# Slots of four samples in place of two, stores of 2 MB in place of 1 MB, and a first round of loads split over two DMA queues

## The chip, the core and the metric

The kernel runs on one core of one Trainium2 chip, in one launch. The metric is device time in microseconds (us). The kernel before was timed in three runs: 326.96, 327.68 and 327.71 us, median 327.68 us.

A core has a matrix engine (TensorE, "PE" in the profile, its weight loads "PEld"), a vector engine ("DVE"), an activation engine ("ACT"), a general engine ("POOL") and a synchronisation engine ("SP"). Here SP and ACT compute nothing: they only wait on semaphores and issue DMA transfers. A transfer issued by SP goes through queue q1 of the profile, one issued by ACT through queue q10. Both queues are worked off by the same 16 DMA engines. Each of the 16 adds one to the transfer's semaphore when its share has landed, so a finished transfer adds 16 (`DMA = 16` in the code).

## The reference

There are 128 samples. Each sample `x[b]` is a float32 matrix of 128 channels by 1024 time steps, 512 KB. A subject number from 0 to 7 picks one of eight 128x128 weight matrices for each sample, and the sample's product with it is added to the sample:

```
w = weights[subjects]                       # (128, 128, 128)
out = x + einsum('bct,bcd->bdt', x, w)      # (128, 128, 1024), float32
```

So 64 MB are read and 64 MB are written, with 512 KB of weights beside them. Every sample is used once.

## The kernel before

**Tiling.** The 128 samples are taken in 64 tiles of `G = 2` samples, 1 MB each. The on-chip memory holds `SLOTS = 23` slots `xs[k]`, one tile each. Tile `i` uses slot `i % 23`. Within a slot the 128 partitions are the channels, and a partition's row holds the two samples' 1024 floats one after the other, 8 KB.

**Loads.** SP first loads all eight weight matrices (L132), then runs over the tiles (L133 to L145) and issues one transfer of 512 KB for each sample. A load is written so that four rows of a sample, 16 KB that lie together in memory, are read as one piece and written into four partitions (`ROWS = 4`, L144). In the first round, from the fourth tile on, SP waits until the tile three places back has landed (`LEAD = 3`, L138). In later rounds SP waits until the slot's earlier tile has been stored (L136). A slot has one semaphore, which counts two loads and one store a round (`TURN`).

**Compute.** For each sample POOL copies the weight matrix that the subject picks into one of four small buffers (L170). For the first sample of a tile, the copy first waits until the vector engine has finished the tile two places back (L169), and until the tile's two loads have landed (L172). Then PE multiplies the sample in two pieces of 512 time steps into one of two PSUM buffers (L177; each float32 matmul shows as two instructions). When both samples of a tile are done, DVE adds the PSUM buffer to the slot in place (L187), 128x2048 elements in one instruction.

**Stores.** ACT waits for the add of tile `i` (L188) and issues one transfer of 1 MB for it (L189 to L194): 128 rows of 8 KB, each of which goes to two places in memory, 4 KB for each sample. The order of the work on every engine is the order written in the source; there is no planner. The two loops are written one after the other, but each engine only sees its own instructions, so SP runs ahead as far as its waits and its queue let it. At the end SP waits until the last 23 stores have landed (L197, L198).

The helper `transfer` (L52) issues every load and store, so that in the profile all of them bear its line, L59.

Of the kernel before, what the change touches and what calls it, by code (L numbers as in the profile page):

```python
# [1 line left out]

# [4 lines left out]

F32 = mybir.dt.float32
I32 = mybir.dt.int32
ALU = mybir.AluOpType


G = 2  # L30

N = 512

SLOTS = 23

W_SLOTS = 4
P_SLOTS = 2

R = 8
DMA = 16  # L40

TURN = DMA * (G + 1)

LEAD = 3

IDLE = 3

ROWS = 4
QUEUES = {mybir.EngineType.SP: "qSPDynamicHW", mybir.EngineType.Activation: "qActDynamicHW"}


def transfer(nc, engine, out, in_):  # L52

    later, nc._always_lower_symbolic_ap = nc._always_lower_symbolic_ap, False
    ins, outs = engine.lower_ap_dma(in_), engine.lower_ap_dma(out)
    nc._always_lower_symbolic_ap = later
    return engine.add_instruction(  # L59
        mybir.InstDMACopy(  # L60
            name=nc.get_next_instruction_name(),
            engine=engine.engine,
            ins=ins,
            outs=outs,
            mode="Copy",
            cce_op=ALU.bypass,
            queue=QUEUES[engine.engine],
        )
    )


@with_exitstack
def kernel(
    ctx: ExitStack,
    tc: tile.TileContext,
    x: bass.AP,
    subjects: bass.AP,
    weights: bass.AP,
    out: bass.AP,
):  # L80
    nc = tc.nc
    B, C, T = x.shape
    S, _, D = weights.shape
    NT = B // G

    def sbuf(name, *shape, dtype=F32):
        return ctx.enter_context(nc.sbuf_tensor(name, list(shape), dtype)).ap()

    given, near, wrap, index = (
        sbuf(name, 1, B, dtype=I32) for name in ("given", "near", "wrap", "index")  # L90
    )
    w_all = sbuf("w_all", C, S, D)
    ws = [sbuf(f"w{i}", C, 1, D) for i in range(W_SLOTS)]
    zeros = sbuf("zeros", C, N)
    xs = [sbuf(f"x{i}", C, G, T) for i in range(SLOTS)]
    ps = [
        ctx.enter_context(nc.psum_tensor(f"ps{i}", [D, G, T], F32)).ap() for i in range(P_SLOTS)
    ]

    s_given = tc.alloc_semaphore("s_given")  # L100
    s_wall = tc.alloc_semaphore("s_wall")
    s_index = tc.alloc_semaphore("s_index")
    s_zeros = tc.alloc_semaphore("s_zeros")
    s_copied = tc.alloc_semaphore("s_copied")
    s_product = tc.alloc_semaphore("s_product")
    s_added = tc.alloc_semaphore("s_added")
    s_slot = [tc.alloc_semaphore(f"s_slot{i}") for i in range(SLOTS)]

    with tc.tile_critical():  # L109

        nc.scalar.dma_start(given, subjects.rearrange("(o b) -> o b", o=1)).then_inc(s_given, DMA)

        nc.vector.memset(zeros, 0.0).then_inc(s_zeros, 1)  # L113
        nc.tensor.wait_ge(s_zeros, 1)
        for _ in range(IDLE):
            nc.tensor.matmul(  # L116
                ps[P_SLOTS - 1][:, G - 1, :N], zeros[:, :D], zeros, start=True, stop=True
            )

        nc.vector.wait_ge(s_given, DMA)
        nc.vector.tensor_scalar(near, given, -S, S - 1, ALU.max, ALU.min).then_inc(s_index, 1)  # L123
        nc.vector.wait_ge(s_index, 1)
        nc.vector.tensor_scalar(wrap, near, 0, S, ALU.is_lt, ALU.mult).then_inc(s_index, 1)  # L125
        nc.vector.wait_ge(s_index, 2)
        nc.vector.tensor_tensor(index, near, wrap, ALU.add).then_inc(s_index, 1)  # L127
        nc.gpsimd.wait_ge(s_index, 3)

        nc.sync.dma_start(w_all, weights.rearrange("s c d -> c s d")).then_inc(s_wall, DMA)  # L132
        for i in range(NT):  # L133
            k, turn = i % SLOTS, i // SLOTS
            if turn:
                nc.sync.wait_ge(s_slot[k], TURN * turn)  # L136
            elif i >= LEAD:
                nc.sync.wait_ge(s_slot[k - LEAD], DMA * G)  # L138
            for g in range(G):
                transfer(  # L140
                    nc,
                    nc.sync,
                    xs[k][:, g, :],
                    x[i * G + g].rearrange("(a r) t -> a (r t)", r=ROWS),  # L144
                ).then_inc(s_slot[k], DMA)  # L145

        nc.gpsimd.wait_ge(s_wall, DMA)
        for i in range(NT):
            k, turn = i % SLOTS, i // SLOTS
            loaded = TURN * turn + DMA * G  # L150
            p = ps[i % P_SLOTS]

            if i < P_SLOTS:
                nc.tensor.wait_ge(s_slot[k], loaded)
            for g in range(G):
                b = i * G + g
                if b % R == 0:
                    _, subject = nc.values_load_multi_w_load_instructions(  # L160
                        index[0:1, b : b + R],
                        engines=[mybir.EngineType.Pool],
                        min_val=0,
                        max_val=S - 1,
                        skip_runtime_bounds_check_because="the index is clamped on the chip above",
                    )
                w = ws[b % W_SLOTS]
                if i >= P_SLOTS and g == 0:
                    nc.gpsimd.wait_ge(s_added, i - P_SLOTS + 1)  # L169
                copy = nc.gpsimd.tensor_copy(w, w_all[:, bass.ds(subject[b % R], 1), :])  # L170
                if i >= P_SLOTS and g == 0:
                    copy.wait_op(s_slot[k], loaded, "sem-ge")  # L172
                copy.then_inc(s_copied, 1)

                nc.tensor.wait_ge(s_copied, b + 1)
                for t in range(0, T, N):
                    mm = nc.tensor.matmul(  # L177
                        p[:, g, t : t + N],
                        w[:, 0, :],
                        xs[k][:, g, t : t + N],  # L180
                        start=True,
                        stop=True,
                    )
                mm.then_inc(s_product, 1)

            nc.vector.wait_ge(s_product, (i + 1) * G)
            nc.vector.tensor_tensor(xs[k], p, xs[k], ALU.add).then_inc(s_added, 1)  # L187
            nc.scalar.wait_ge(s_added, i + 1)  # L188
            transfer(  # L189
                nc,  # L190
                nc.scalar,
                out[i * G : (i + 1) * G].rearrange("g d t -> d g t"),
                xs[k].rearrange("d (o g) t -> d o (g t)", o=1),
            ).then_inc(s_slot[k], DMA)  # L194


        for i in range(NT - SLOTS, NT):  # L197
            nc.sync.wait_ge(s_slot[i % SLOTS], TURN * (i // SLOTS + 1))  # L198


# [1 line left out]
_INS = ["x", "itok_B_0_7", "L0_cond_weights"]  # L202
_OUTS = [((128, 128, 1024), "float32")]


# [20 lines left out]
```

## Time and profile before

| | |
|---|---|
| median of three runs | 327.68 us |
| the profiled execution's own time | 327.88 us |
| its span, from first to last instruction | 326.0 us |
| PE busy | 239.9 us (74%) |
| DVE busy | 147.9 us (45%) |
| POOL busy | 34.4 us (11%) |
| queue q1 (SP): packets, bytes, share of the engines' time | 7184, 67.64 MB, 49.6% |
| queue q10 (ACT): packets, bytes, share of the engines' time | 9218, 67.11 MB, 49.1% |
| one load, median from issue to landing | 11.8 us |
| one store, median from issue to landing | 42.4 us |

The span is cut by the profile into 40 equal slices of 8.15 us; for each slice it gives the busy share of the engines and of the 16 DMA engines in tenths, and the bytes moved in GB/s. The same numbers can be asked of the trace for any stretch of time. A packet is what a DMA engine moves in one go; the small packets of 4 bytes that raise a semaphore are counted too. Times inside the execution, such as "at 276 us", count from the start of the span. MB and GB in the profile are decimal; the "512 KB" and "2 MB" of a transfer are 524,288 and 2,097,152 bytes.

### The profile page before, as it was taken

The page shows a single profiled execution, that of the slowest core. Times are in us where ns is not written, and L with a number is a line of the kernel's source. Part 1 is how long each engine was busy: PE and PEld are TensorE (multiplying, and loading weights), DVE is VectorE, ACT ScalarE, POOL GpSimd, SP SyncE. Part 2 cuts the span into 40 slices and gives each one's busy share as a digit, 9 for nine tenths or more (in the row PEclk, how much of TensorE's full clock was granted, in tenths as well). Part 3 has the DMA queues.
Part 4 walks back from the last instruction along what each step waited for, and adds up shares of the span by engine and source line. Part 5 has one row for each costly group of instructions (what it writes and reads, how often), then busy time and mean ns, then how long its engine had stood idle before and what let it go on. Part 6 is the DMA issues. An engine that isn't in the chain of part 4 may idle for free.

```text
span 326.0 us, 1641 instructions
## 1 busy us (share of the span) xinstructions
PE 239.9 (74%) x518; PEld 95.3 (29%) x518; DVE 147.9 (45%) x68; POOL 34.4 (11%) x132
## 2 busy tenths in 40 slices
PE   5999999889898897899988988986866777000000
PEld 2444444333333332333333333332322322000000
DVE  1267667555555554555555555554354354100000
POOL 1011111111111111011111111111011010000000
PEclk9799999999999999999999999999999999555555
DMA  7999999999999999999999999999999999999993
GB/s 257 416 415 423 429 426 420 421 422 428 420 424 429 421 428 419 427 424 425 425 425 427 417 424 423 429 428 419 425 429 433 420 417 427 425 425 427 424 428 167
DMA packets 16410, 134.85 MB, mean 414 GB/s; under 512 B 3089, under 2 KB 4114, under 8 KB 4114
## 3 DMA queue, kind: packets, MB, share of 16 engines
q1 hardware_dynamic: 7184, 67.64, 49.6%
q10 hardware_dynamic: 9218, 67.11, 49.1%
q8 instruction: 4, 0.07, 0.1%
q14 instruction: 4, 0.03, 0.0%
HBM read 67.63 MB, written 67.11 MB: 413 GB/s over the span
## 4 chain that ended last, share of the span: by engine, by line
PE 43%; DVE 19%; issue 18%; POOL 2%; DMA 2%; POOLq 1%; SPq 0%
PE ps L177 43%; DVE x L187 19%; POOL w L170 2%; DMA x<-in_x_dram 2%; POOLq L170 1%; SPq L59 0%; SPq L132 0%; SPq L222 0%; SPq L109 0%
## 5 line engine op out<-in xcount | busy, mean ns | idle before, releaser
L177 PE MATMUL ps<-x,w 128*128 128x512 f32 x512 | 235.3, 606 | 34.5 <-POOL w L170 32.5
L187 DVE TENSOR_TENSOR x<-ps,x 128x2048 f32<-128x2048 f32 x64 | 146.7, 2292 | 128.7 <-PE ps L177 128.7
L177 PEld LDWEIGHTS ps<-x,w 128*128 128x128 f32 x512 | 93.6, 191 | 176.2 <-issue 95.8
L170 POOL COPY w<-w_all 128x128 f32 x128 | 34.2, 297 | 237.9 <-DMA x<-in_x_dram 197.1
L116 PE MATMUL ps<-zeros 128*128 128x512 f32 x6 | 4.6, 922 | 1.7 <-DVE zeros L113 1.7
L116 PEld LDWEIGHTS ps<-zeros 128*128 128x128 f32 x6 | 1.7, 304 | 3.7 <-issue 2.1
L113 DVE MEMSET zeros<- 128x512 f32 x1 | 0.5, 485 | 1.1 <-SPq L109 1.1
L123 DVE TENSOR_SCALAR near<-given 1x128 int32<-1x128 int32 x1 | 0.2, 215 | 0.6 <-DMA given<-in_itok_B_dram 0.6
L127 DVE CUSTOM_DVE_ANT_0 index<-near,wrap 1x256 uint16<-1x256 uint16 x1 | 0.3, 280 | 0.0
L125 DVE TENSOR_SCALAR wrap<-near 1x128 int32<-1x128 int32 x1 | 0.2, 215 | 0.0
L213 POOL MEMSET const-float32-0.0<- 128x1 f32 x1 | 0.1, 100 | 0.2 <-issue 0.2
L213 POOL MEMSET const-bfloat16-1.0<- 128x1 bf16 x1 | 0.1, 103 | 0.0
L213 POOL MEMSET const-uint8-127<- 128x1 uint8 x1 | 0.1, 102 | 0.0
L213 POOL MEMSET const-float32-1.0<- 128x1 f32 x1 | 0.1, 100 | 0.0
## 6 DMA issues: line engine op xcount, KB each, us to landing
x<-in_x_dram SPq DMA_DIRECT2D x128, 512.0 KB, 11.8
out_dram<-x ACTq DMA_DIRECT2D x64, 1024.0 KB, 42.4
w_all<-in_L_cond_weights_dram SPq DMA_DIRECT2D x1, 512.0 KB, 4.2
given<-in_itok_B_dram ACTq DMA_DIRECT2D x1, 0.5 KB
```

What stands on the lines that cost most here:

```text
L113: nc.vector.memset(zeros, 0.0).then_inc(s_zeros, 1)
L116: nc.tensor.matmul(ps[P_SLOTS - 1][:, G - 1, :N], zeros[:, :D], zeros, start=True, stop=True)
L123: nc.vector.tensor_scalar(near, given, -S, S - 1, ALU.max, ALU.min).then_inc(s_index, 1)
L125: nc.vector.tensor_scalar(wrap, near, 0, S, ALU.is_lt, ALU.mult).then_inc(s_index, 1)
L127: nc.vector.tensor_tensor(index, near, wrap, ALU.add).then_inc(s_index, 1)
L170: copy = nc.gpsimd.tensor_copy(w, w_all[:, bass.ds(subject[b % R], 1), :])
L177: mm = nc.tensor.matmul(p[:, g, t : t + N], w[:, 0, :], xs[k][:, g, t : t + N], start=True, stop=True,)
L187: nc.vector.tensor_tensor(xs[k], p, xs[k], ALU.add).then_inc(s_added, 1)
L213: nc = _bacc.Bacc("TRN2", target_bir_lowering=False, num_devices=1)
```

## The change

A slot now holds four samples (`H = 2` halves of `G = 2`), and there are 12 slots: 24 MB in place of 23. A partition's row in a slot is 16 KB. There are 32 slot fillings in place of 64.

Compute stays in halves of two samples: 64 groups of matmuls and 64 adds of 128x2048 elements, in the same order, with the same two PSUM buffers.

Stores: the first slot filling is stored in its two halves, 1 MB each; every later one in a single transfer of 2 MB, issued when its second half has been added. So there are 33 stores in place of 64. A row of the 2 MB store is 16 KB and goes to four places of 4 KB.

Loads: still one transfer of 512 KB for each sample. In the first round SP loads all four samples of slot 0, and only three samples of slots 1 to 11. The fourth samples of those eleven slots are loaded by ACT: two as soon as the weights have landed, one after each half store of slot 0, then two after each later store until none is left. The wait that kept SP at most three tiles ahead in the first round (`LEAD`) is gone. In later rounds SP loads all four samples after the slot's store has landed.

Semaphores: a slot has two, one for each half. A load counts for its half, a store for the second half (for the first filling also for the first).

```diff
-SLOTS = 23
+H = 2
+SLOTS = 12
-TURN = DMA * (G + 1)
-LEAD = 3
...
-    NT = B // G
+    NT = B // (G * H)
...
-    xs = [sbuf(f"x{i}", C, G, T) for i in range(SLOTS)]
+    xs = [sbuf(f"x{i}", C, H * G, T) for i in range(SLOTS)]
...
-    s_slot = [tc.alloc_semaphore(f"s_slot{i}") for i in range(SLOTS)]
+    s_pair = [[tc.alloc_semaphore(f"s_pair{i}_{h}") for h in range(H)] for i in range(SLOTS)]
+
+    def emptied(i, h):
+        turns = i // SLOTS
+        loads = DMA * G * turns
+        if h == H - 1:
+            return loads + DMA * turns
+        return loads + (DMA if i and i % SLOTS == 0 else 0)
+
+    def loaded(i, h):
+        return emptied(i, h) + DMA * G
+
+    def load(engine, i, q):
+        k, h = i % SLOTS, q // G
+        transfer(
+            nc,
+            engine,
+            xs[k][:, q, :],
+            x[i * H * G + q].rearrange("(a r) t -> a (r t)", r=ROWS),
+        ).then_inc(s_pair[k][h], DMA)
+
+    def store(i, q0, q1):
+        k, b = i % SLOTS, i * H * G
+        transfer(
+            nc,
+            nc.scalar,
+            out[b + q0 : b + q1].rearrange("g d t -> d g t"),
+            xs[k][:, q0:q1, :].rearrange("d (o g) t -> d o (g t)", o=1),
+        ).then_inc(s_pair[k][(q1 - 1) // G], DMA)
...
         for i in range(NT):
-            k, turn = i % SLOTS, i // SLOTS
-            if turn:
-                nc.sync.wait_ge(s_slot[k], TURN * turn)
-            elif i >= LEAD:
-                nc.sync.wait_ge(s_slot[k - LEAD], DMA * G)
-            for g in range(G):
-                transfer(
...
+            k = i % SLOTS
+            if i >= SLOTS:
+                nc.sync.wait_ge(s_pair[k][H - 1], emptied(i, H - 1))
+                if k == 0:
+                    nc.sync.wait_ge(s_pair[k][0], emptied(i, 0))
+            for q in range(H * G - (1 if 0 < i < SLOTS else 0)):
+                load(nc.sync, i, q)
+
+        shared = list(range(1, SLOTS))
+
+        def share(count):
+            for _ in range(count):
+                if shared:
+                    load(nc.scalar, shared.pop(0), H * G - 1)
+
+        nc.scalar.wait_ge(s_wall, DMA)
+        share(2)
...
-        for i in range(NT):
+        for j in range(NT * H):
+            i, h = j // H, j % H
+            k = i % SLOTS
+            p = ps[j % P_SLOTS]
+            mine = xs[k][:, h * G : (h + 1) * G, :]
...
-            nc.vector.tensor_tensor(xs[k], p, xs[k], ALU.add).then_inc(s_added, 1)
-            nc.scalar.wait_ge(s_added, i + 1)
-            transfer(
...
+            nc.vector.tensor_tensor(mine, p, mine, ALU.add).then_inc(s_added, 1)
+
+            if i == 0 or h == H - 1:
+                nc.scalar.wait_ge(s_added, j + 1)
+                store(i, h * G if i == 0 else 0, (h + 1) * G)
+                share(1 if i == 0 else 2)
```

The waits of POOL, PE and DVE are the same as before, with `j` for the tile's number and the half's semaphore for the slot's; the last waits of SP cover the last 12 stores.

## The prediction

> **What bounds the kernel now.** I read the page first: busy shares, slices, queues.
>
> ```profile
> PE   5999999889898897899988988986866777000000
> DMA  7999999999999999999999999999999999999993
> GB/s 257 416 415 423 429 426 420 421 422 428 420 424 429 421 428 419 427 424 425 425 425 427 417 424 423 429 428 419 425 429 433 420 417 427 425 425 427 424 428 167
> q1 hardware_dynamic: 7184, 67.64, 49.6%
> q10 hardware_dynamic: 9218, 67.11, 49.1%
> ```
>
> The DMA engines are full from the second slice to the last but one, at about 425 GB/s; PE stops six slices before the end. The bound is bytes: 134.85 MB at 0.425 MB/us is 317 us of the 326. The rest is the start (the first slice) and the landing at the end. The packet counts tell the packet sizes: a load is 32 packets of 16 KB and 16 small ones for the semaphore, (32+16)x128 = 6144, and the weights (1024 rows and 16) make 7184. A 1 MB store is 128 packets of 8 KB and 16 small ones: 144x64 = 9216.
>
> Then three stretches in the DMA view: loads alone, both queues full, stores alone.
>
> ```profile
> q1 hardware_dynamic: 522, 5.70, 100.7%
> ...
> q1 hardware_dynamic: 2328, 25.45, 60.4%
> q10 hardware_dynamic: 2329, 16.93, 40.4%
> ...
> q10 hardware_dynamic: 2807, 20.45, 101.4%
> ```
>
> The first line is 5 to 19 us: 407 GB/s. The next two are 100 to 200 us: the queues moved the same number of packets, 2328 and 2329, but not the same bytes. So an engine takes one packet from each queue in turn, small ones included. Three loads (144 packets, 1.5 MB) go with one store (144 packets, 1 MB): 25.45/16.93 = 1.50. The last line is 272 to 320 us: 426 GB/s from stores alone. Because loads win, they run ahead until all 23 slots are full; SP then waits for stores, and at 276 us, when the last add starts, (321-276)x0.425 = 19 MB of stores are still to move. That backlog hides the last tile's compute completely. The timeline prices what it hides (start, duration; the last number is idle time before):
>
> ```profile
> 262.13 0.53 POOL L170 COPY w<-w_all 128x128 f32 x2 [3.69 <-DMA x<-in_x_dram]
> 262.48 3.70 PE L177 MATMUL ps<-x,w 128*128 128x512 f32 x8 [0.52 <-POOL w L170]
> 266.22 2.29 DVE L187 TENSOR_TENSOR x<-ps,x 128x2048 f32<-128x2048 f32 x1 [1.93 <-PE ps L177]
> ```
>
> From a landed pair to its finished add: 268.51-262.13 = 6.4 us.
>
> **What the Trainium skill says.** "DMA: Bandwidth & Descriptors", section "Queues, rings and completion order": each engine goes round the queues that have work, one packet at a time; 2328 against 2329 agrees. Section "Issuing engines are not separate DMA queues": a second issuing engine saves only issue time. True here for the total rate, 424 GB/s with two queues and 426 with one, but the trace shows that the queue and the packet size set who gets the bytes. Section "Bandwidth": the fabric's ceiling is 435 GB/s; 426 is 98% of it, so a better packet form can gain 2% at the very most.
>
> **The change, part by part.**
>
> *Bytes, PE, DVE and POOL work* stay the same: 64 adds of 2.29 us, the same matmuls and copies.
>
> *Packets.* A store's row is 16 KB in one piece on chip, and the loads show that a 16 KB piece travels as one packet, so I take a 2 MB store as 128+16 packets. That removes 31x144 = 4464 packets, 279 on each engine. No row prices one. The skill's section "Why small descriptors are slow" gives about 3 cycles of overhead a packet, and its bandwidth section 850 MHz: 3.5 ns, an estimate of 1.0 us. Lower bound: nothing, since loads in 16 KB packets (407 GB/s) show no better rate than 8 KB stores (426). Upper bound, if stores reach the ceiling: 67 MB at 435 in place of 426 GB/s is 3.3 us. I take -0.7.
>
> *The start.* Two loads on ACT's queue at 5 us run beside SP's: 4 loads, 2.1 MB, at 425 in place of 407 GB/s: -0.2 us. They may delay the second pair of slot 0 by 2 us, but PE needs it only after its first group, which at the start takes 13.6-8.2 = 5.4 us. With `LEAD` gone SP fills its queue earlier; the order of loads is the same, so nothing.
>
> *Who gets the bytes.* This decides. 144 packets of a 2 MB store now go with three loads, 2.10 against 1.57 MB: a round is 3.67/0.425 = 8.64 us, and stores win. So the backlog no longer grows; does any remain at the end?
>
> - Fill. PE sets the pace of compute: two adds start at 13.61 and 17.04 us, 3.43 us apart, so filling 4 is added by 16+9x3.43 = 47 us; the ACT queue, full from the first store's first packet (19.9 us before: queue q10 moved one packet between 15 and 20 us), is not empty. It works off two 1 MB halves (each with three loads: 2.62/0.425 = 6.2 us), nine shared loads (each beside one of SP's: 2.5 us) and stores 1 to 4 (8.64 each): 12.3+22.2+34.5 = 69 us, done at 89. SP meanwhile: about 10 loads before 19.9, then 6+9+12 = 37 in all, 4+11x3. Both finish the fill together.
> - After it. Store n ends at 89+8.64(n-4), so store 11 starts at 141. Loads come at 3 in 8.64 us: filling n is loaded at 89+11.52(n-11). From its last packet to its store's first packet I count 0.6 (landing: before, q1's last packet moved by 271.5 us and the copy that waited for it started at 271.99) +6.4+1.1 (the weights' issue at 0.96 to first bytes at 2.1) = 8.2 us. Filling 11 is ready at 97, its store's turn comes at 141: a lag of 44 us, and each filling takes 11.52-8.64 = 2.88 off it. It is gone after 15 fillings, at the 26th of 0 to 31, about 264 us. From there stores wait for compute, a filling takes 4.19/0.425 = 9.87 us, and the last load ends at 264+4.8x9.87 = 311 us. SP never lacks a slot in this: stores are ahead.
> - The end. Filling 30 was loaded at 311-9.9 = 301.5, its store starts at 309.7 and by 311.4 has 4/7 of the rate: 0.4 MB. The remaining 1.7 MB keep the engines busy until 315.4. Store 31 can start at 311.4+8.2 = 319.6. The engines stand idle for 4.2 us, then move 2.1 MB alone in 4.9. If store 30 starts later, as the first store of before did behind queued loads (issued 15.93, first bytes 19.9, that is 4.0 in place of 1.1 us), idle is 1.2+2.1 = 3.3. If both last steps took 4 us: about 6. I take +4.2.
>
> This idle time is what the 19 MB hid before. Queued behind the last waits: ACT's last store stands behind the last add, and SP's final wait behind its landing. Earlier ACT waits for adds hold up shared loads queued behind them; PE then gets a pair up to 2 us late, hidden by four or five stores in the queue. If that cover were gone it would be DMA idle time.
>
> *Sum:* +4.2-0.2-0.7 = +3.3 us on the profiled execution's 326.0 span (327.88 with what lies around it): 329.3. The profiled execution is 0.2 above the median, so the median goes to 327.68+3.3 = 331.0. The landing after the last packets (span end less 321) is kept as it is.
>
> **Rivals.**
>
> 1. *The backlog lasts* (not slower). If the lag of 44 us at the end of the fill were over 60, or the gain of stores 2 us a filling in place of 2.88, two stores would still be queued at the end and the last compute is hidden: 327.68-0.9 = 326.8, and down to 325 with the full packet gain. For it: the lag is a difference of long sums. Against: five fillings of margin. The same follows if a 2 MB store travels in 8 KB packets (272 packets): then 5.7 loads go with a store, loads win as now, all 12 slots fill. Against that: loads already travel in 16 KB packets.
> 2. *A longer end* (slower still). Pairs land late because one engine lags (from 322 to 324 us the DMA share is 0.06, one engine of 16, working off its last stores alone), and a pair waits for the slowest of 16, then the last store once more. Price: 2 to 3 us more idle, 333 to 335.
> 3. *16 KB stores to four places are slower in memory.* 1% on stores is 1.6 us. Nothing in the profile speaks for it; loads, which also write four pieces of 4 KB, run 4% slower alone, but beside stores not.
>
> **How the numbers follow.** Idle end as worked out: 0.66, 329 to 333. Backlog lasts, by either way: 0.20, 325 to 327.6, about half of it on each side of the line for faster. Longer end or slower stores: 0.14, 333 to 336. A measurement can tell about 0.3%, 1 us: faster is below 326.7, slower above 328.7. The low end of the first case, with the full packet gain, adds a little to "same" and "faster". So 0.14 faster, 0.14 same, 0.72 slower. The range that leaves out a tenth on either side: 326.4 to 334.
>
> **What would show it.** Right: packets on q10 fall to about 4,750 plus 530 for shared loads; in a middle stretch (120 to 220 us) both queues have equal packets but q10 has 4/3 of q1's bytes; loads go on until about 311 us instead of 271; PE works into the last 15 us; a slice near the end shows the DMA engines idle; a store's time from issue to landing falls to about 10 us late in the run. Wrong: about 9,000 packets on q10, or PE ending before 300 us with the DMA row full to the end. If the rate in the middle is above 430 GB/s, the packet price was too low.

## The result, and the profile after

The changed kernel takes 330.61 us (median of five runs, 330.49 to 331.40) beside 327.14 us for the kernel before in the same session: a ratio of 1.0102, with a 95% interval of 1.0091 to 1.0114. That is 3.5 us slower by the medians, 3.3 by the ratio. The forecast was 331.0. The profiled execution spans 329.6 us, 3.6 more than before; it is the slowest of the five (331.40 us).

The page of the changed kernel, the same rows as were shown of before:

```profile
PE   5999987999987687776767676767676768767750
DMA  7999999999999999999999999999999999999856
GB/s 241 422 409 428 421 418 426 421 424 422 424 425 427 426 427 425 424 429 425 425 426 433 424 421 431 419 429 429 424 429 422 427 427 422 431 418 429 354 229 254
q10 hardware_dynamic: 5282, 72.88, 52.2%
q1 hardware_dynamic: 6656, 61.87, 45.1%
```

PE used to stop six slices before the end; now it works into the last slice but one. The DMA row used to be full up to the last slice but one; now the last three slices are at 8, 5 and 6 tenths, 354, 229 and 254 GB/s. The 5282 packets on q10 are the 33 stores at 144 packets, 4752, the 11 shared loads at 48, 528, and two of the subject numbers' load: a 2 MB store does travel in 128 packets of 16 KB.

Who got the bytes, from 120 to 220 us of the changed kernel (queue: packets, MB, share of the engines' time):

```profile
q10 hardware_dynamic: 1674, 24.33, 57.3%
q1 hardware_dynamic: 1674, 18.25, 43.2%
```

The packets are equal to the last one. The bytes are 4 to 3 for the stores, where before they were 3 to 2 for the loads (25.45 and 16.93 MB from 100 to 200 us). This is what drains the backlog. When it is gone can be read from the same view in stretches of 10 us, here 240 to 250 and 250 to 260 us:

```profile
q10 hardware_dynamic: 164, 2.42, 57.1%
q1 hardware_dynamic: 162, 1.82, 43.0%
...
q1 hardware_dynamic: 203, 2.20, 52.0%
q10 hardware_dynamic: 143, 2.08, 49.0%
```

Up to 250 us the stores have packets in every turn; after it they have not, and loads move 203 packets beside 143. From there on every store waits for its own add.

The end, by stretches (start:end, length, busy of PE, PEld, DVE, POOL, granted clock, DMA share, GB/s) and then the last pair's instructions in time:

```profile
310.00:314.00 4.00, 3.56 (x8) 1.44 (x8) 1.49 (x1) 0.53 (x2) 1.00 0.66 279
314.00:318.00 4.00, 2.77 (x7) 1.25 (x7) 2.29 (x1) 0.53 (x2) 1.00 0.87 369
318.00:322.00 4.00, 1.08 (x3) 0.19 (x1) 2.29 (x1) 0.00 (x0) 1.00 0.02 8
322.00:328.00 6.00, 0.00 (x0) 0.00 (x0) 0.00 (x0) 0.00 (x0) 0.51 0.83 350
```

```profile
315.03 0.53 POOL L206 COPY w<-w_all 128x128 f32 x2 [4.40 <-DMA x<-in_x_dram]
315.38 3.70 PE L213 MATMUL ps<-x,w 128*128 128x512 f32 x8 [1.23 <-POOL w L206]
319.11 2.29 DVE L223 TENSOR_TENSOR x<-ps,x 128x2048 f32<-128x2048 f32 x1 [2.64 <-PE ps L213]
```

The last pair of samples lands at 315.0 us: the copy that waits for it starts then. Copy, matmuls and add take the 6.4 us that they took before, until 321.4. By 318 the store ahead has been moved, and from 318 to 322 us the DMA engines do next to nothing (share 0.02). Then the last 2 MB go alone. Before, the same 6.4 us ended at 278.4 with stores queued up to 324.

### The profile page after: what moved, and what is told of

Same layout as the page of the kernel before. It is cut to its first block, busy times and chain, and to the rows that moved or that the text cites. A ratio compares the mean times of both kernels' runs of the same rounds, so it can differ in the third digit from the quotient of the medians.

```text
span 329.6 us, 1607 instructions
## 1 busy us (share of the span) xinstructions
PE 251.9 (76%) x518; PEld 101.4 (31%) x518; DVE 147.9 (45%) x68; POOL 34.4 (10%) x132
## 2 busy tenths in 40 slices
DMA packets 11946, 134.85 MB, mean 409 GB/s; under 512 B 2593, under 2 KB 3618, under 8 KB 3618
## 3 DMA queue, kind: packets, MB, share of 16 engines
q10 hardware_dynamic: 5282, 72.88, 52.2%
## 4 chain that ended last, share of the span: by engine, by line
PE 45%; issue 34%; DVE 13%; POOL 2%; DMA 2%; POOLq 1%; SPq 0%
PE ps L213 45%; DVE x L223 13%; POOL w L206 2%; DMA x<-in_x_dram 2%; POOLq L206 1%; POOLq L196 0%; SPq L58 0%; SPq L161 0%; SPq L256 0%; SPq L139 0%
## 5 line engine op out<-in xcount | busy, mean ns | idle before, releaser
L213 PE MATMUL ps<-x,w 128*128 128x512 f32 x512 | 247.6, 636 | 65.5 <-POOL w L206 62.4
L213 PEld LDWEIGHTS ps<-x,w 128*128 128x128 f32 x512 | 99.8, 202 | 213.3 <-issue 107.4
```

The lines of the kernel that those rows point to most:

```text
L213: mm = nc.tensor.matmul(p[:, g, t : t + N], w[:, 0, :], xs[k][:, h * G + g, t : t + N], start=True, stop=True,)
```

## The experiments

Two theories stand against each other. The *turn theory* is that of the prediction: engines take one packet from each queue in turn, 16 KB store packets let the stores overtake, and the last compute stands open at the end. The *rival* is that something in the new form costs all through the run: stores of 2 MB in 16 KB rows, 12 slots of four samples, or loads on two queues. The kernel before ran beside every experiment, so gains are reckoned from the ratios: 0.1% is 0.33 us, and the change costs 1.02%, 3.3 us.

**Packet size alone (e1_8k).** Everything of the changed kernel stays: transfers, waits, slots. Only the on-chip side of a 2 MB store is described as two rows of 8 KB.

```diff
-            xs[k][:, q0:q1, :].rearrange("d (o g) t -> d o (g t)", o=1),
+            xs[k][:, q0:q1, :].rearrange("d (o g) t -> d o (g t)", o=(q1 - q0) // G),
```

> The changed kernel, with each 2 MB store's on-chip row described as two pieces of 8 KB in place of one of 16 KB; transfers, waits and slots stay. Turn theory (an engine takes one packet from each queue in turn, so 16 KB store packets let the stores overtake, the backlog is gone at the end and the last compute stands open): about 9,250 packets on q10, in the middle loads get 272/48 = 5.7 transfers (2.97 MB) beside each store (2.10 MB), a ratio of 1.42; the last load ends before 285 us, the DMA row is full to the end, 326.8 to 327.8 us. Rival (2 MB stores, 12 coarse slots, or loads on two queues cost by themselves): 330 to 331 us, as the changed kernel.

327.79 us, ratio to before 1.0014 (1.0007 to 1.002). From its page:

```profile
PE   6899976989698999999995897959869598000000
DMA  7999999999999999999999999999999999999994
q10 hardware_dynamic: 9250, 72.88, 53.2%
```

The queues from 120 to 220 us:

```profile
q1 hardware_dynamic: 1957, 21.47, 50.9%
q10 hardware_dynamic: 2731, 21.06, 50.1%
```

The stretch from 310 to 318 us, where the changed kernel began to fall idle:

```profile
310.00:318.00 8.00, 0.00 (x0) 0.00 (x0) 0.00 (x0) 0.00 (x0) 0.50 1.01 426
```

9250 packets on q10, as worked out. In this middle stretch the bytes are nearly equal and not 1.42 to 1, because the loads had run ahead until the slots were full. What SP waited for from 120 to 220 us (us in total, times, longest):

```profile
SPq L58 <- DMA out_dram<-x: 78.2, 10, 9.6
```

The changed kernel's SP never waits for a slot. The ratio of 1.42 itself shows in the next experiment, where slots stay free. Here PE stops six slices before the end, the DMA row is full up to the last slice, and 2.9 us of the 3.3 are gone. The large stores, the 12 slots and the shared loads are all still there, so what they cost together, beside any gain of theirs, is the remaining 0.14%.

**The packets late in the run (e9_late8k).** The same 8 KB rows, but only for the stores of fillings 20 to 31 (`o=1 if i < 20 else 2`). The first round of loads and the stores of fillings 0 to 19 are those of the changed kernel.

> The changed kernel, with the stores of fillings 20 to 31 described in rows of 8 KB in place of 16 KB; fillings 0 to 19 as in the changed kernel. Turn theory: until filling 20 the lag of the stores falls to about 15 us; from there 5.7 loads go with each store, the lag grows by 3.5 us a filling to some 50 us, the last load ends before 300 us and the last compute is hidden: 326.7 to 327.6 us. If what counts is how far behind the stores were in the fill, and not the packets at the end: 330 us or more.

327.58 us, 1.0002 (0.9994 to 1.001). From 120 to 220 us, and from 230 to 290 us:

```profile
q10 hardware_dynamic: 1700, 24.13, 56.9%
q1 hardware_dynamic: 1695, 18.45, 43.7%
...
q1 hardware_dynamic: 1366, 14.91, 58.9%
q10 hardware_dynamic: 1368, 10.55, 41.9%
```

The balance turns with the packet size, stores ahead and then loads ahead, within one run. In both stretches the packets are equal within a few; in the second the bytes are 1.41 to 1 for the loads, where 1.42 follows from equal turns. The last add starts at 301.1 us and the loss is gone. So what decides is whether a backlog is there at the end, not how far behind the stores were in the first round.

**No shared loads (e4_noshare).** All loads of the first round on SP.

```diff
-            for q in range(H * G - (1 if 0 < i < SLOTS else 0)):
+            for q in range(H * G):
...
-        shared = list(range(1, SLOTS))
+        shared = []
```

> The changed kernel with all loads of the first round on SP, none on ACT. Turn theory: the stores overtake far earlier (about filling 8, near 95 us), stay level with compute from there, and the end is the same open compute: 330 to 331 us. Rival (loads on ACT's queue are what costs, by holding up stores and pairs): 327 to 328.5 us.

330.97 us, 1.0106 (1.0089 to 1.0123). The queues from 40 to 80 and from 60 to 90 us:

```profile
q10 hardware_dynamic: 645, 9.50, 56.0%
q1 hardware_dynamic: 688, 7.49, 44.3%
...
q1 hardware_dynamic: 612, 6.69, 53.1%
q10 hardware_dynamic: 414, 6.00, 47.1%
```

The end, by stretches:

```profile
318.00:322.00 4.00, 0.74 (x2) 0.00 (x0) 2.29 (x1) 0.00 (x0) 1.00 0.01 4
322.00:328.00 6.00, 0.00 (x0) 0.00 (x0) 0.00 (x0) 0.00 (x0) 0.63 0.83 350
```

The stores are level with compute by 90 us in place of 250, and the end is the same: hardly any bytes from 318 to 322 us, and the same time. The shared loads delay the moment at which the backlog is gone, by 160 us, but not past the end. They are not what costs.

**A later start of the stores (e5_hold).** The kernel of e4 with one wait changed: `nc.scalar.wait_ge(s_added, max(j + 1, HOLD))` with `HOLD = 12`, so that no store goes before the 12th add.

> The kernel without shared loads (all first-round loads on SP), with one wait changed: ACT issues no store before the 12th add (six fillings), about 52 us, in place of 14 us. Packets, transfers and slots stay. Turn theory: with the stores 38 us further behind at the start, about 72 us at the end of the fill, the 2.9 us a filling do not close the lag by filling 31; some 15 us of stores are left when the last load lands, the DMA row is full to the end, and the open compute is gone. The longer stretch with loads alone, at 407 in place of 425 GB/s, costs 1.5 us. So 327.5 to 328.8 us, less than the same kernel without the wait (330.97). Rival (2 MB stores or coarse slots cost by themselves): 331 to 333 us, as a later start can only add.

327.32 us, 1.0001 (0.9992 to 1.0009): 1.05% or 3.4 us less than the same kernel without the delay. The queues from 19 to 52 us (loads alone) and from 270 to 300:

```profile
q1 hardware_dynamic: 1240, 13.52, 100.9%
...
q10 hardware_dynamic: 499, 7.26, 57.0%
q1 hardware_dynamic: 500, 5.47, 43.2%
```

The end, by stretches:

```profile
310.00:318.00 8.00, 3.27 (x6) 1.00 (x4) 2.29 (x1) 0.00 (x0) 0.71 0.93 393
318.00:322.00 4.00, 0.00 (x0) 0.00 (x0) 0.00 (x0) 0.00 (x0) 0.50 0.96 406
```

At 270 to 300 us the stores still win 4 to 3, which means that they still had a backlog. The last add ends at 315.6 and the engines are never empty for a stretch (the 0.93 and 0.96 are engines that finish at different times: by the trace's semaphore events, the sixteen shares of the last store but one landed from 316.0 to 318.9 us). Packets, slots and transfer sizes are those of the slow kernel; holding stores back for 38 us made it faster. Together with e4, which has no loads on two queues and is as slow as the changed kernel, this rules the rival out. It came out below its range (327.5 to 328.8), and its trace has a part of the reason: from 5 to 52 us it moved 19.27 MB where the kernel before moved 19.70, which at 425 GB/s is 1.0 us lost and not 1.5, and from 90 to 250 us it moved 68.20 where that one moved 67.94, 0.6 us gained.

**The end itself (e3_split_last and e8_fine_end).** In e3 the last filling is stored in two halves of 1 MB, each after its add.

```diff
-            if i == 0 or h == H - 1:
+            if i in (0, NT - 1) or h == H - 1:
                 nc.scalar.wait_ge(s_added, j + 1)
-                store(i, h * G if i == 0 else 0, (h + 1) * G)
+                store(i, h * G if i in (0, NT - 1) else 0, (h + 1) * G)
...
+        nc.sync.wait_ge(s_pair[(NT - 1) % SLOTS][0], loaded(NT - 1, 0) + DMA)
```

The added line at the bottom lets SP wait for the first half's store too.

> The changed kernel with the last slot filling stored in two halves of 1 MB, each when its half is added. If the idle stretch before the last store sets the end: the first half moves in that stretch and the last transfer is 1 MB in place of 2 MB, so 2.4 us less, 328.0 to 328.5 us, with the stretch before the last half still there. If the 3.3 us come from the run as a whole: at most 0.5 us less, 330 us or more.

328.26 us, 1.0028 (1.0016 to 1.0041). The end of e3:

```profile
318.00:320.00 2.00, 0.16 (x1) 0.00 (x0) 1.80 (x1) 0.00 (x0) 1.00 0.69 283
320.00:322.00 2.00, 0.00 (x0) 0.00 (x0) 0.49 (x1) 0.00 (x0) 1.00 0.19 78
322.00:324.00 2.00, 0.00 (x0) 0.00 (x0) 0.00 (x0) 0.00 (x0) 0.62 1.02 422
```

The first half fills most of the gap, and 0.74% or 2.4 us are gone, the time of a 1 MB transfer. In e8 the last two samples are also waited for, multiplied, added and stored one by one.

> The changed kernel with a finer end: the last filling's first half is stored by itself, its last two samples are loaded, multiplied, added and stored one by one. From the last landing to the last store's first packet that leaves about 4.3 us (copy 0.3, two matmuls of one sample 1.9, add of 1024 columns 1.2, issue 0.9), covered by 1.5 MB of other stores (3.7 us), and a last transfer of 0.5 MB. If the open compute is the whole loss: 326.2 to 327.4 us, level with the kernel before or better. If something else in the run costs 1 us or more: 328 us or more.

327.61 us, 1.0007 (0.9999 to 1.0015): level with before, 0.2 us above the range. The open end is thus 3.1 of the 3.3 us. The middle of the run stays as in the changed kernel (1676 and 1674 packets, 24.31 and 18.27 MB from 120 to 220 us), so a drained backlog by itself costs nothing that these runs can tell; the open end does.

**The lead wait (e6_before_nolead).** The kernel before without the two lines of `LEAD`.

> The kernel before without its lead wait: in the first round SP issues loads as fast as its queue takes them. If the slower start of the changed kernel (397 in place of 407 GB/s between 5 and 19 us) comes from SP's deeper queue: the same here, 390 to 400 GB/s and 0.3 to 0.6 us more. If it comes from loads on two queues: 407 GB/s and no difference from before beyond 0.2 us.

327.47 us, 1.0002 (0.9993 to 1.001). Its profiled execution moved 5.52 MB from 5 to 19 us (394 GB/s), the kernel before 5.70 (407), the changed one 5.55 (397). But e4 and e5, both with SP's queue just as deep and no shared loads, moved 5.52 MB (394 GB/s) and 5.74 MB (410 GB/s) in that stretch. Neither explanation fits both, and no difference in time is left to explain. The start varies from run to run by about 0.5 us of transfer, and why stays open.

**32 KB loads (e2_rows8 and e7_before_rows8).** With `ROWS = 8` a load is 16 packets of 32 KB. This should have let the loads win against 16 KB stores.

> The changed kernel with ROWS = 8 in place of 4: a load is 16 packets of 32 KB in place of 32 of 16 KB; stores stay at 16 KB packets. Turn theory: 144 packets of a store now go with 144/32 = 4.5 loads, 2.36 against 2.10 MB, a ratio of 1.13 for the loads; the backlog stays, the last load ends by about 290 us, the end is full, 326.0 to 327.2 us. Rival (16 KB stores of 2 MB are slow by themselves): 330 us or more.

360.4 us, 1.098 (1.0958 to 1.1002): far outside its range. Its time says nothing of the turns, because these loads are slow. Its trace does agree with them: from 120 to 220 us q1 and q10 moved 1266 and 1269 packets, 20.68 and 18.53 MB, 1.12 to 1 where 1.13 was expected. The same edit in the kernel before shows the slow loads without shared loads or large stores:

> The kernel before with loads in 16 packets of 32 KB in place of 32 of 16 KB (ROWS = 8). The changed kernel with such loads took 360 us, with 225 GB/s between 5 and 19 us. If the 32 KB loads are slow by themselves: below 300 GB/s between 5 and 19 us here too, and 340 us or more. If it takes loads on both queues: above 395 GB/s there and 327 to 329 us.

389.32 us in a single run. Loads alone, 5 to 19 us:

```profile
q1 hardware_dynamic: 198, 3.24, 97.2%
```

3.24 MB in place of 5.70: 232 GB/s. So it is this form of the load itself; what in it is slow was not tested.

**An attempt to beat both (e10_hold9_fine).** No shared loads, no store before the 9th add, and the finer end.

> An attempt to beat both kernels: no shared loads, no store before the 9th add (about 42 us in place of the 52 us of the longer hold), and the finer end (the last filling stored as 1 MB, 0.5 MB and 0.5 MB). The shorter stretch with loads alone saves 0.4 us against the longer hold (327.32); the lag of the stores runs out within the last two fillings, where the finer end leaves at most 1 us open. 326.5 to 327.3 us. If the lag runs out earlier: as the finer end alone, 327.6 us.

327.24 us, 0.9998 (0.999 to 1.0007): within its range, but no different from before, so it beats the changed kernel only. The kernels that keep their engines busy to the end arrive at 327.2 to 327.8 us; all move the same 134.85 MB.

## Why the prediction was right

*What bounds the kernel.* The bytes, and the rate of 425 GB/s, held: 426 in the middle of the changed kernel.

*Packets.* The form was right, 5282 packets. The gain of 0.7 us came out lower in this execution. From 90 to 250 us the kernel before moved 67.94 MB and the changed one 68.15: 0.21 MB, or 0.5 us. From 5 to 19 and from 19.9 to 89 us it moved less, 5.55 for 5.70 and 29.16 for 29.29 MB: 0.28 MB, 0.7 us lost. So the two small gains of the sum (0.2 at the start, 0.7 for packets) came to about nothing. The start term had the wrong sign in this execution; e4 and e5 show that the start varies by as much without shared loads.

*Who gets the bytes.* The ratio of 4 to 3 was exact. The lag was to be gone at filling 26, near 264 us; it was gone near 250. That is 14 us early on a lag of 44, which does no harm once the backlog is gone at all, and it says that the margin of the first rival's estimate was more than five fillings.

*The end.* The last load was put at 311.4 and the last store's first packet at 319.6. The pair landed at 315.0 and the last store moved from about 322. What SP's queue still moved from 311.4 to 318 us:

```profile
q1 hardware_dynamic: 6, 0.05, 1.8%
```

So the loads as a whole did end at 311.4; six packets were late. By the trace's semaphore events, the sixteen shares of the last load landed from 307.1 to 315.0 us. The estimate took the 16 engines as one, and a pair waits for the slowest: the others ran out of work earlier (share 0.66 from 310 to 314 us). But a wait at this point also brings the engines level. Before, the shares of the last store landed from 320.6 to 324.5 us; now they land from 327.9 to 328.1. So the 2 to 3 us of the second rival came, and were returned at the end. Whether the late engine is the same in both kernels is not shown. Reckoned as length times the share that is missing from 1, the engines' unused time from 310 to 329.6 us is 1.4+0.5+3.9+1.0+1.6 = 8.4 us, and before, from 320 to 326, it was 4.9: 3.5 us, where 4.2 were predicted.

*The sum.* 4.2-0.9 = 3.3 was predicted, 3.6 of span and 3.5 us of time were measured: the open end was sized 0.7 us too large and the gains 0.9 too large. The mechanism held, but that the sum fits this closely is luck: two errors of opposite sign nearly cancel.

*A store's time near the end* was put at about 10 us from issue to landing; the median of stores issued from 272 to 320 us is 13.3. A likely reason is that a store starts behind loads that already wait in the engines, as the first store of before did; no run tests it.

*The rivals.* That the backlog lasts is what e1, e5 and e9 make true by force, and their 327.3 to 327.8 us is where it was priced (326.8), a little above. That 16 KB stores are slow in memory is refuted by the 426 GB/s.

## What to carry to other kernels

In these runs two queues that both had work waiting shared the DMA engines packet by packet, so the size of their packets set the split: count packets, semaphore packets included, before changing the form of a transfer. Here a backlog of stores at the end hid the last tile's compute; a change that lets the stores catch up takes it away, and then most of the last tile's path lies open. If the backlog is gone, make the end fine (here two 1 MB stores for one of 2 MB gave back 2.4 of 3.3 us), or keep stores back early.

## What the runs showed of the hardware that was not expected

- Loads whose rows in memory are taken as 16 pieces of 32 KB run at 232 GB/s alone, where 32 pieces of 16 KB run at 407 (5 to 19 us of the kernel before in both forms, the slow one run once). The cause was not looked for.
- The 4-byte packets that raise semaphores take a full turn: with them counted, 2328 and 2329, 1674 and 1674 packets come out equal; with data packets alone they would not, since a load has 16 small ones beside 32 large and a store 16 beside 128.
- A doubled store packet changes the rate little: 425 and 426 GB/s from 90 to 250 us.
- The 16 engines drift apart: the shares of the last load of the changed kernel landed over 7.9 us (307.1 to 315.0), those of the last load before over 0.5 (271.4 to 271.9).
